# Four graph layers on one core: scales loaded first, a series on GpSimd, a direct spread, a branch hint and new ranks

## The chip, the cores and the metric

The kernel runs on one core of a Trainium2 chip. A core has a TensorE (PE) for matrix products, a VectorE (DVE), a ScalarE (ACT), a GpSimd (POOL) and a SyncE (SP); they run side by side, each through its own list of instructions in order, and wait for each other by semaphores. Operands lie in SBUF, products of the PE go to PSUM, and transfers between DRAM and SBUF are issued by SP or POOL. The metric is the time of one execution in microseconds (us) on the device.

## The reference

There are 4096 nodes with 64 features `x`, and an adjacency matrix `adj` of 4096 x 4096 with entries 0 and 1 (about 32 ones in a row). Four layers follow, and each adds its result to `x`; ahead of each the features go through a layer norm and a relu:

```python
h = max(layernorm(x), 0)
# layer 0: a decaying sum over the last 100 neighbours of each node
rank = cumsum(adj != 0, axis=1); k = min(rank[:, -1:], 100)
x += (mask * where(pos > 0, 0.5 ** (k - pos), 0)) @ (h @ W) + b      # pos = rank - (deg - k)
# layer 1: hyperbolic attention; lorentz_linear = linear map, sigmoid(first) * exp(scale) + 1.1, a rescaling
att = adj * sigmoid((2 + 2 * (qm @ k.T)) / att_scale + att_bias)
x += normalised(att @ lorentz_linear(h))
# layer 2: two gated steps, each m = adj @ (x @ W), then a GRU cell (sigmoid, sigmoid, tanh), then relu
# layer 3: hyperbolic midpoint: num = adj @ (gamma * X), den = adj @ (gamma - 1),
#          then artanh, a scaling by the row's sum, tanh, and relu in the tangent space
```

## The kernel before

`fast_kernel` (L916) assumes entries of 0 and 1 and tests that they are; `general_kernel` (L39) computes any input. After the fast kernel has written its output, its flag is loaded on every engine, and `tc.If(others > 0)` (L1910) runs the general kernel if an assumption did not hold. With these inputs it does not run: every engine branches over it.

**Tiles.** The nodes stand in 4 quarters (`q`) of 1024 and in 32 row blocks (`b`) of 128. The adjacency, transposed, is loaded once by POOL's queue and turned into an 8-bit float on the way: 65 transfers `A<-in_adjT`, seven ahead, 256 KB each when they land, and it stays in SBUF for all four layers.

**Who sets the order.** `Plan` (L636) collects operations with a cost per engine, what they need, what they write, and a rank (`prio`). `Plan.order` (L790) then runs through time as a model: at each step it takes, on the engine that can begin earliest, the operation with the lowest rank, and it chooses between ACT and DVE where both are allowed. Its constants (`HOP`, `FROM_PE`, `SWITCH`, `NEAR`, `WAIT`, `TURN`, `LOAD` and others, from L640) are the model's hops between engines and penalties; the dictionary `K` (L912) holds ranks and a few counts. The result is written out under `tc.manual_schedule()` (L1825), so on the chip each engine works in that order, whatever the real times are.

**Layer 0** (`layer0`, `block0`, L1215 and L1231). The rank of a neighbour is counted in PSUM: each row block adds a triangle matrix times its 128 x 1024 piece of the adjacency (`tri`, operand `ftri`), and a second product (`upd`, `fupd`) completes the count. Between the two, `weigh` reads the counts and makes the decaying weights from them, on ACT (L1275) or DVE (L1277). A quarter's block is done in two halves of 512 columns, so two chains count, weigh, update, count run side by side: 4 x 32 x 2 = 256 weighs in all. A third product (`add`) sums the features with the weights. All products are issued from one helper line, L1047; transposes from L1056.

**Layer 1** (`pre1`, `open1`, `stream1`, `post1`). `pre1` makes the vectors, the keys and the queries of a quarter, transposed. The 128 x 512 queries are written to DRAM (`qS`, `qs<-m`) and `open1` reads them back in four transfers, so that each half of the features lies on both halves of the partitions. `stream1` then goes over 16 pairs of row blocks: a score is eight products into one PSUM tile of 128 x 1024, ACT takes the sigmoid (L1025), DVE multiplies by the adjacency (L983), and PE adds the products. `es` (the exponentials of the scales), `att_mul` and `att_add` come from a slice `scales` of the constants `W`. `W` (456.5 KB) is loaded by SP after some adjacency transfers; `later_consts` (L1130) then computes them and `deep`, a value that the tests need, and the gates' biases.

**Layers 2 and 3.** `stream2` and `gates` do the two gated steps. `pre3` prepares layer 3, `stream3` (L1666) sums over the neighbours for a unit of half a quarter (four column blocks, eight units), and `post3` (L1686) finishes the units in the groups (0, 1, 2), (3, 4, 5), (6, 7). `kept` units have the first two quarters' sum taken early by `kept3` and the rest later. Powers (inverse roots) run on POOL (`root`, L1010). `artanh2` (L1584) takes two logarithms on ACT and, for small arguments, a series of six DVE operations; it is called seven times, four in `pre3` and three in `post3`.

**Tests.** All of `adj` is also read as 32-bit floats in 128 transfers of 512 KB and tested to be exactly 0 or 1, by one DVE operation (L1200) or two sigmoids on ACT (L1204, L1205). `K["tests"]` of them are tied to places in layer 1, the others come after it.

Of the kernel before, what the change touches and what calls it, by code (L numbers as in the profile page):

```python
# [9 lines left out]
F32 = mybir.dt.float32  # L10
# [3 lines left out]
ALU = mybir.AluOpType  # L14
# [621 lines left out]
class Plan:  # L636
# [4 lines left out]
    TO_PE = 0.055  # L641
    FROM_PE = 0.21
    SWITCH = 0.11
    TABLE = 1.3
# [3 lines left out]
    FIRST = 1.2  # L648
    NEAR = 0.396
    WAIT = 1.892  # L650
    TURN = 0.355
    LOAD = 0.136

# [121 lines left out]
    def drop(self, b):  # L775
# [7 lines left out]
        elif b.kind != "fixed":  # L783
# [3 lines left out]
            for j in range(b.units):  # L787
                self.ps[i + j] = t

    def order(self, nst):  # L790
        self.nst = nst
# [13 lines left out]
        def est(o, e):  # L805
            t = 0.0
            for d in o.needs:
                hop = (0.0 if d.on == e and not d.nbytes else self.FROM_PE if d.on == "PE" else
                       self.TO_PE if e == "PE" else self.HOP)
                t = max(t, d.end + hop)  # L810
            return t
# [9 lines left out]
        while len(placed) < len(self.ops):  # L821
# [39 lines left out]
            if o.mode:  # L861
                d += self.SWITCH if o.mode != mode else 0.0
                mode = o.mode
# [47 lines left out]

K = {"lags": (32, 32, 32), "two": (0, 1, 2, 3), "p0": (0.779, 0.744, 1.253, 0.665), "p1": (1.588, 1.422, 1.181, 2.145), "ahead": 7, "early": 0, "steps": ((0, 0, 16), (1, 0, 16), (2, 0, 16), (3, 0, 16)), "score": (3.0, 3.0, 2.571, 3.0), "add": (3.1, 3.971, 4.33, 3.215), "p2": ((0.42, 0.267, 0.42, 0.43), (0.48, 0.272, 0.42, 0.204)), "l2": (4.0, 4.857), "l3": 6.0, "tests": 31, "act": 0, "g": (5, 6), "stage": (5, 8), "cnt": 2, "weigh": 0.164, "sum": 1.612, "kept": 4, "units": ((0, 1, 2), (3, 4, 5), (6, 7)), "p3": (0.541, 0.329, 0.157)}  # L912


@with_exitstack
def fast_kernel(ctx: ExitStack, tc: tile.TileContext, t: dict, out: bass.AP, flag: bass.AP):  # L916
# [92 lines left out]

    def root(o, a, power, n=QB, prio=2.0, cost=2.45):  # L1010
        return plan.op({"POOL": cost + 0.157 * (n - QB)},
                       lambda e: G_.tensor_tensor(o.get(), a.get(), POWER[power].get().to_broadcast([P, n]), ALU.pow),  # L1012
                       (a, POWER[power]), (o,), prio)
# [77 lines left out]
    ones16 = const.tile([P, 1], BF16, name="ones16")  # L1091
    tiny = const.tile([P, 1], F32, name="tiny")
    tiny16 = const.tile([P, 2], F16, name="tiny16")
    tiny8 = const.tile([P, 2], F8, name="tiny8")
# [17 lines left out]

    def first_consts():
        V.memset(powers[:, 0:1], -0.5)
        V.memset(powers[:, 1:2], 0.5)
        V.memset(ones, 1.0)
        V.memset(ones16, 1.0)
        V.memset(tiny, TINY)
        V.memset(tiny8.bitcast(U8), 1)
        V.memset(half16, 0.5)  # L1120
        V.memset(mean16, 1.0 / P)
        V.memset(odd, 0.0)
        V.memset(deep[:, 0:1], -DEEP)
        V.memset(deep[:, 1:2], -BIG2 - DEEP)
        after = sb_tiles[NSB - 1][:, P:2 * P]
        V.tensor_scalar(after, diff, 0.0, None, op0=ALU.is_gt)
        V.scalar_tensor_tensor(tri, ident, 256.0 - MAX_NEIGH, after, op0=ALU.mult, op1=ALU.add)
        V.tensor_scalar(upd, tri, -1.0, 1.0, op0=ALU.mult, op1=ALU.add)

    def later_consts():  # L1130
        S_.activation(es, w("scales", 0, 3), AF.Exp)
        S_.activation(deep[:, 2:3], deep[:, 0:1], AF.Sigmoid)
        V.reciprocal(deep[:, 2:3], deep[:, 2:3])
        V.reciprocal(att_mul, w("scales", 4, 5))
        V.tensor_scalar(att_mul, att_mul, 2.0, None, op0=ALU.mult)
        V.tensor_tensor(att_add, att_mul, w("scales", 3, 4), ALU.add)
        for i in (1, 2):
            V.tensor_tensor(gate_b[:, 3 * i - 3:3 * i - 1], w(f"gb{i}", 0, 2), w(f"gb{i}", 3, 5), ALU.add)
            V.tensor_scalar(gate_b[:, 3 * i - 1:3 * i], gate_b[:, 3 * i - 2:3 * i - 1], -1.0, None, op0=ALU.mult)
# [162 lines left out]

    S1, kT, qS = {}, {}, {}

    def pre1(q, prio):
# [70 lines left out]
        qT = sb(2, "qT")  # L1376
        copy(qT, turn4(flat(y), prio), prio=prio)
        d = dram.tile([P, CW], F32, name=f"qs{q}")
        qS[q] = fixed(d)
# [7 lines left out]
    def open1(q):  # L1387
        qd = []
        for c in range(2):
            v = sb(2, "qd")  # L1390
            for r in range(2):
                half = slice(r * D, (r + 1) * D)
                dma(v.part(r)[half, :], View(qS[q].buf, lambda c=c: qS[q].get()[c * D:(c + 1) * D, :]), D * CW * 4, 1.0,
                    after=ends.get(("qd", q), ()))
            qd.append(v)
        return qd, [bank("acc1")] if q < EARLY else [bank("acc") for _ in range(2)]

    def stream1(q, qd, acc, steps):
        early = len(acc) == 1
        for i in steps:  # L1400
            gs = []
            for c in range(2):
                ps = bank("sc", 2)

                def score(e, i=i, c=c, ps=ps):
                    kb = kT[i // 4].get()[:, (i % 4) * P:(i % 4 + 1) * P]
                    o = ps.get().rearrange("p (j n) -> p j n", j=2)
                    for h in range(2):
                        for j in range(2):
                            half = slice(j * D, (j + 1) * D)  # L1410
                            mm(o[h * D:(h + 1) * D, j, :], kb[half, h * D:(h + 1) * D], qd[c].get()[half, :])
                scores.append(plan.op({"PE": 0.856}, score, (kT[i // 4], qd[c]), (ps,), K["score"][q], "corner", after=scores[-1:]))
                g = sb(4, "g")
                fn(g, ps, AF.Sigmoid, 1280, 1.0, "sig", View(attv.buf, lambda: att_add), View(attv.buf, lambda: att_mul))
                g3 = g.re("p (j n) -> p j n", j=2)
                m = g.re("p (k n) -> p k n", n=P)
                tt(m, m, A[q][i].bits(U8).re("p j (k c n) -> p c (j k) n", c=2, n=P)[:, c], ALU.mult, 2 * CW, 1.0)
                gs.append(g3)
            for j in range(2):
                def add(e, i=i, j=j, gs=gs):  # L1420
# [6 lines left out]
                    for r in range(2):  # L1427
                        half = slice(r * D, (r + 1) * D)
                        for c in range(2):
                            mm(acc[r].get()[c * D:(c + 1) * D, :], s[half, :], gs[c].get()[half, j, :], b == 0, b == NB - 1)  # L1430
                ends[1, q, i] = plan.op({"PE": 0.856}, add, (*gs, S1[(2 * i) // QB]), tuple(acc), K['add'][q],
                                           "narrow" if early else "corner")

    def post1(q, acc, prio):
# [13 lines left out]
        r = stat()  # L1448
        root(r, s, -0.5, prio=prio, cost=1.9)
        v = nodes("att")  # L1450
        tt(v, sup, rows(r), ALU.mult, prio=prio)
        tt(X[q], X[q], v, ALU.add, prio=prio)
        g = nodes("g0")
        relu_ln(X[q], g, prio, 1.9)
        HL[0, q] = two(f"hl0_{q}")
# [127 lines left out]

    def artanh2(x, n, prio):  # L1584

# [5 lines left out]
        x2 = stat(n)  # L1591
        tt(x2, xc, xc, ALU.mult, n, prio)
        p = stat(n)
        ts(p, x2, 2.0 / 9, None, ALU.mult, n=n, prio=prio)
        for k in (7, 5, 3):
            stt(p, p, 2.0 / k, x2, ALU.add, ALU.mult, n, prio)
        stt(p, p, 2.0, xc, ALU.add, ALU.mult, n, prio)
        low = stat(n).bits(I32)
        ts(low, xc, 0.18, None, ALU.is_lt, n=n, prio=prio)
        tt(q, up, q, ALU.subtract, n, prio)  # L1600
# [85 lines left out]
    def post3(units, banks, kept, prio):  # L1686
# [35 lines left out]
        tt(n, n, rd, ALU.mult, nb, prio)  # L1722
        a = artanh2(n, nb, prio)
        part = stat(nb)
# [16 lines left out]

    plan.op({"POOL": 0.75}, lambda e: pool_consts(), (), (identv,), 1.0)
    plan.op({"DVE": 1.2}, lambda e: first_consts(), (identv,), (triv, pv), 0.0)

# [11 lines left out]
    def load_consts(after, behind):  # L1756
        gate(Wv, lambda: W[:1, :1], behind)
        dma(Wv, View(None, lambda: t["consts"][:, :L.at["scales"].stop]), P * L.at["scales"].stop * 4, 0.1, after=after)
        for q in range(NQ):
            bias0(q)  # L1760
        plan.op({"DVE": 1.5}, lambda e: later_consts(), (Wv,), (esv, attv, gbv), 3.0)
        subnormals(3.0)
# [26 lines left out]
    for k, (b, q) in enumerate(left):  # L1789
        if k < early:  # L1790
            turn = 2 + k * (NQ * NB // 2 - 2) // early
            turn = (ends[1, turn // (NB // 2), turn % (NB // 2)],)
            later_test(b, q, turn, {"DVE": 1.31, "ACT": 2.35} if k % 8 < K["act"] else {"DVE": 1.31})
        else:
            later_test(b, q, (ends[1, NQ - 1, NB // 2 - 1],), {"DVE": 1.31, "ACT": 2.35})

# [3 lines left out]
    def verdict(e):  # L1800
# [11 lines left out]
        V.tensor_scalar(both.get(), both.get(), float(n), None, op0=ALU.not_equal)  # L1812
    plan.op({"DVE": 1.4}, verdict, (*tested_, esv), (both,), 0.2)
    keys = [-1, -3, *range(NQ * NB), *(f"g{q}" for q in range(NQ)), *(f"n{us[0]}" for us in K["units"])]
# [4 lines left out]
    def count_odd(e):  # L1819
        mm(fl.get()[:1, :1], total.get(), ones, True, False)  # L1820
        mm(fl.get()[:1, :1], both.get(), ones, False, True)
    plan.op({"PE": 0.2}, count_odd, (total, both), (fl,), 0.2, "full")
    plan.op({"DVE": 0.2}, lambda e: V.tensor_copy(flag, fl.get()[:1, :1]), (fl,), (), 0.2)

    with tc.manual_schedule():  # L1825
        for o in plan.order(NST):
            o.emit(o.on)
    return plan
# [85 lines left out]
```

## Time and profile before

| | |
|---|---|
| runs of the kernel | median 654.51 us (654.39 to 654.60, 3 runs) |
| the profiled execution | 654.29 us, span 652.5 us |
| mean granted TensorE clock | 0.986 |
| busy, share of the span | PE 604.3 us (93%), DVE 518.7 (79%), ACT 432.2 (66%), POOL 123.7 (19%) |
| DMA | 93.6 MB in 33020 packets, mean 143 GB/s |

The profile shows one execution: for every instruction its engine, its line and its duration, and for idle time the instruction or transfer whose end released the engine. The span goes from the first instruction to the last. "Busy" counts an engine's work and not its waits. "PE" is the matrix products and "PEld" the loading of their weights, which overlaps them. A release is inferred from the semaphore that came last. SPq, DVEq and the like are the sequencers of the engines, which issue transfers and take branches.

### The profile page before, as it was taken

Reading aid. Unit: us, or ns where it says so; the run is one execution under the profiler, and the core shown is the slowest. Engines: PE = TensorE matmul, PEld = TensorE weight load, DVE = VectorE, ACT = ScalarE, POOL = GpSimd, SP = SyncE. Lnnn points to the kernel's source line nnn. Section 1 sums busy time; section 2 is a strip of 40 time slices with the busy share of each in tenths; the row PEclk is TensorE's granted clock in tenths of the full one; section 3 lists DMA queues with packets and bytes.
Section 4 is the critical chain, followed back from the end, with each engine's and each line's share of the span. In section 5 each row is a group of like instructions: output and inputs, shape, how many; then the busy total and the mean of one; then the engine's idle time right before and its main releaser. Section 6 shows DMA issues by size and latency. Waiting matters only on the chain.

```text
span 652.5 us, 15178 instructions
## 1 busy us (share of the span) xinstructions
PE 604.3 (93%) x6236; PEld 320.6 (49%) x6236; DVE 518.7 (79%) x969; ACT 432.2 (66%) x646; POOL 123.7 (19%) x126
## 2 busy tenths in 40 slices
PE   4879999999999999999999999999999999999970
PEld 2646666666643333333333333454444445589970
DVE  5855667766678999998989898888888889887765
ACT  4756676777757667766766666448534999988543
POOL 5422342523113101100110110020000213330222
PEclk9989999999999999999999999999999999999995
DMA  8999999999311242123225242698999886636301
GB/s 111 145 108 107 108 115 136 107 120 107 40 49 33 81 131 66 66 81 114 65 71 142 59 124 69 192 355 297 345 339 328 286 298 220 213 102 205 131 26 45
DMA packets 33020, 93.60 MB, mean 143 GB/s; under 512 B 3888, under 2 KB 4656, under 8 KB 32944
## 3 DMA queue, kind: packets, MB, share of 16 engines
q1 hardware_dynamic: 23584, 75.78, 35.4%
q0 software_dynamic: 9360, 16.78, 25.8%
q8 instruction: 51, 0.84, 0.5%
q14 instruction: 25, 0.20, 0.1%
HBM read 138.68 MB, written 2.10 MB: 216 GB/s over the span
## 4 chain that ended last, share of the span: by engine, by line
PE 78%; DVE 9%; ACT 6%; DMA 3%; issue 2%; POOL 1%; DVEq 0%; ACTq 0%; SPq 0%; POOLq 0%
PE p L1047 75%; ACT m L1275 4%; DVE m L1277 3%; PE p L1056 3%; DVE m L983 2%; ACT m L1025 2%; DMA m<-in_x_pm 1%; DVE m L1000 1%; POOL s L1012 1%; DMA m<-in_adjT 1%; DVE s L1005 1%; DMA A<-in_adjT 1%; DVE s L1000 0%; ACT junk L1204 0%; DVE s L983 0%
## 5 line engine op out<-in xcount | busy, mean ns | idle before, releaser
L1047 PE MATMUL p<-m,m 64*64 64x512 f32 (+2 forms) x2538 | 318.8, 555 | 0.6 <-ACT m L1025 0.4
L1025 ACT ACTIVATE m<-p,fatt_add,fatt_mul 128x1024 f32<-128x1024 f32 x128 | 149.8, 1201 | 68.9 <-PE p L1047 66.6
L1012 POOL TENSOR_TENSOR s<-s,powers 128x8 f32<-128x8 f32 (+1 forms) x46 | 87.1, 1903 | 465.7 <-DVE s L994 209.5
L983 DVE TENSOR_TENSOR m<-m,A 128x1024 f32<-128x1024 f32 x128 | 152.8, 1221 | 16.9 <-ACT m L1025 16.2
L1047 PEld LDWEIGHTS p<-m,m 64*64 64x64 f32 x2072 | 79.1, 132 | 145.0 <-issue 97.4
L1275 ACT ACTIVATE m<-p 128x512 int16<-128x512 int8 x168 | 97.3, 596 | 56.8 <-PE p L1047 53.2
L1200 DVE SCALAR_TENSOR_TENSOR junk<-m 128x1024 uint8<-128x1024 f32 x97 | 118.4, 1220 | 1.9 <-DMA m<-in_adjT 0.6
L1047 PEld LDWEIGHTS <-m 128*64 128x64 f16 x1536 | 87.8, 110 | 61.7 <-issue 13.3
L1047 PE MATMUL p<-A,m 128*64 128x512 fp8e4 x1024 | 115.2, 380 | 0.0
L1277 DVE TENSOR_SCALAR m<-p 128x512 int16<-128x512 int8 x88 | 60.5, 690 | 40.3 <-PE p L1047 38.8
L1047 PE MATMUL p<-A,fupd 128*64 128x256 f16 x496 | 71.6, 288 | 15.7 <-ACT m L1275 6.6
L1047 PEld LDWEIGHTS <-fupd 128*64 128x64 bf16 x496 | 46.9, 111 | 58.5 <-issue 46.4
L1047 PE MATMUL p<-A,ftri 128*64 128x256 f16 x512 | 72.5, 281 | 3.0 <-DMA A<-in_adjT 3.0
L1047 PE MATMUL p<-m,A 128*128 128x132 f16 x1024 | 62.5, 220 | 4.6 <-ACT m L1025 3.0
L1047 PEld LDWEIGHTS <-A 128*128 128x128 fp8e4 x1024 | 60.3, 96 | 8.1 <-issue 8.0
L1025 ACT ACTIVATE m<-m 128x512 f32<-128x512 f32 (+4 forms) x69 | 38.9, 580 | 15.6 <-DVE m L983 10.8
L1025 ACT ACTIVATE m<-p 128x512 f32<-128x512 f32 (+4 forms) x40 | 19.2, 485 | 44.3 <-PE p L1047 39.1
L1005 DVE TENSOR_REDUCE s<-m 128x8 f32<-128x512 f32 (+2 forms) x62 | 42.9, 694 | 4.0 <-DMA m<-in_x_pm 2.0
L1043 POOL DMA_DIRECT2D A<-in_adjT x65 | 35.4, 554 | 30.6 <-DMA A<-in_adjT 29.8
L1047 PEld LDWEIGHTS <-ftri 128*64 128x64 bf16 x512 | 34.8, 111 | 6.7 <-issue 4.4
L1204 ACT ACTIVATE junk<-m,deep 128x1024 uint8<-128x1024 f32 x31 | 35.4, 1143 | 2.6 <-DVE junk L1200 2.5
L1205 ACT ACTIVATE junk<-m,deep 128x1024 uint8<-128x1024 f32 x31 | 35.6, 1149 | 1.0
(106 smaller groups left out, 358.3 us busy)
## 6 DMA issues: line engine op xcount, KB each, us to landing
m<-in_adjT SPq DMA_DIRECT2D x128, 512.0 KB, 5.6
A<-in_adjT POOLq DMA_DIRECT2D x63, 256.0 KB, 17.9
m<-qs SPq DMA_DIRECT2D x16, 128.0 KB, 4.7
m<-m SPq DMA_DIRECT2D x16, 128.0 KB, 4.8
m<-in_x_pm SPq DMA_DIRECT2D x4, 256.0 KB, 7.5
qs<-m SPq DMA_DIRECT2D x4, 256.0 KB, 5.0
out_x<-m SPq DMA_DIRECT2D x3, 256.0 KB, 2.1
m<-in_consts SPq DMA_DIRECT2D x2, 256.0 KB, 3.2
```

Of the source, the lines that this page charges most:

```text
L983: return plan.op(cost or {"DVE": dve(n)}, lambda e: ENG[e].tensor_tensor(o.get(), a.get(), b.get(), op), (a, b), (o,), prio)
L1005: return plan.op({"DVE": dve(n)}, lambda e: V.tensor_reduce(o.get(), a.get(), AX.X, ALU.add), (a,), (o,), prio)
L1012: lambda e: G_.tensor_tensor(o.get(), a.get(), POWER[power].get().to_broadcast([P, n]), ALU.pow),
L1025: S_.activation(o.get(), a.get(), func, **k)
L1043: return plan.op({eng: 0.06 if eng == "SP" else 0.55}, lambda e: ENG[e].dma_start(o.get(), a.get()), (a,), (o,), prio, nbytes=nbytes, afte ...
L1047: nc.tensor.matmul(o, lhsT, rhs, start=start, stop=stop, skip_group_check=True)
L1056: nc.tensor.transpose(o[:, j * P:(j + 1) * P], s[:, j * P:(j + 1) * P], ident)
L1200: V.scalar_tensor_tensor(junk, s.get(), 0.0, s.get(), op0=ALU.not_equal, op1=ALU.not_equal, accum_out=odd[:, i:i + 1])
L1204: S_.activation(junk2, s.get(), AF.Sigmoid, bias=deep[:, 0:1], scale=-BIG0, accum_out=zeros[:, k:k + 1])
L1205: S_.activation(junk2, s.get(), AF.Sigmoid, bias=deep[:, 1:2], scale=BIG2, accum_out=ones_of[:, k:k + 1])
L1275: S_.activation(o, s, AF.Relu, scale=-128.0)
L1277: V.tensor_scalar(o, s, -128.0, 0.0, op0=ALU.mult, op1=ALU.max)
```

## The change

Five things are changed.

1. **Scales first.** The five columns of scales have an SBUF tile of their own and an SP transfer ahead of all others. The constants are made in other groups: `plain_consts` (memsets), `first_consts` (`tri`, `upd`), `scale_consts` (ACT: the exponential and a sigmoid), `other_consts` (DVE: `deep`, `att_mul`, `att_add`) and `gate_consts` (the biases, still after `W`). One more activation, an exponential into `deep[:, 3:4]`, stands ahead of them.
2. **The series of `artanh2` on GpSimd.** Nine small POOL operations in place of six on DVE, in all seven calls (`K["series"]`).
3. **Queries of quarter 0 spread directly**, by four transfers from SBUF to SBUF, without the DRAM tile (`K["direct"]`). The other quarters go by DRAM as before.
4. **A branch hint.** The plan is written out in two parts, and between them, ahead of one DVE operation of the last artanh, each engine gets a hint that the branch of the `If` named "general" is likely taken.
5. **The planner's constants and ranks** have new values: hops from PE and mode switches by kind, `NEAR`, `WAIT`, `LOAD`; nearly all ranks in `K`; early tests 26 instead of 31, one in eight of them allowed on ACT; `kept` from unit 5 on instead of 4; the cost it takes for `root` 1.8 instead of 2.45. The flag's product (`count_odd`) comes after all of `stream3`. With `half` at (0, 0) the attention's sigmoid and product stay whole.

```diff
-    FROM_PE = 0.21
-    SWITCH = 0.11
+    FROM_PE = {"n": 0.22, "f": 0.23, "c": 0.31}
+    TO_DVE = 0.07
+    SWITCH = {"fn": 0.11, "nf": 0.11, "fc": 0.14, "cf": 0.11, "cn": 0.16, "nc": 0.1}
...
-    NEAR = 0.396
-    WAIT = 1.892
+    NEAR = 0.377
+    WAIT = 2.312
     TURN = 0.355
-    LOAD = 0.136
+    LOAD = 0.0
...
-K = {"lags": (32, 32, 32), "two": (0, 1, 2, 3), "p0": (0.779, 0.744, 1.253, 0.665), "p1": (1.588, 1.422, 1.181, 2.145), "ahead": 7, "early": 0, "steps": ((0, 0, 16), (1, 0, 16), (2, 0, 16), (3, 0, 16)), "score": (3.0, 3.0, 2.571, 3.0), "add": (3.1, 3.971, 4.33, 3.215), "p2": ((0.42, 0.267, 0.42, 0.43), (0.48, 0.272, 0.42, 0.204)), "l2": (4.0, 4.857), "l3": 6.0, "tests": 31, "act": 0, "g": (5, 6), "stage": (5, 8), "cnt": 2, "weigh": 0.164, "sum": 1.612, "kept": 4, "units": ((0, 1, 2), (3, 4, 5), (6, 7)), "p3": (0.541, 0.329, 0.157)}
+K = {"lags": (32, 32, 32), "two": (0, 1, 2, 3), "p0": (1.395, 2.467, 1.194, 0.878), "p1": (1.588, 2.782, 1.98, 2.145), "ahead": 7, "early": 0, "steps": ((0, 0, 16), (1, 0, 16), (2, 0, 16), (3, 0, 16)), "score": (3.0, 2.67, 2.571, 1.915), "add": (3.044, 3.971, 3.193, 3.818), "p2": ((0.42, 0.267, 0.42, 0.43), (0.245, 0.272, 0.42, 0.204)), "l2": (4.46, 4.857), "l3": 5.448, "tests": 26, "act": 1, "g": (5, 6), "stage": (5, 8), "cnt": 2, "weigh": 0.05, "sum": 3.161, "kept": 5, "units": ((0, 1, 2), (3, 4, 5), (6, 7)), "p3": (0.294, 0.187, 0.416), "direct": (0,), "half": (0, 0), "soft": (1.661, 1.0, 1.0, 1.622), "series": 1}
...
-    def later_consts():
-        S_.activation(es, w("scales", 0, 3), AF.Exp)
+    def scale_consts():
+        S_.activation(es, scales[:, 0:3], AF.Exp)
         S_.activation(deep[:, 2:3], deep[:, 0:1], AF.Sigmoid)
...
+    def spread(rows_of, prio, after=()):
+        qd = []
+        for c in range(2):
+            v = sb(2, "qd")
+            for r in range(2):
+                dma(v.part(r)[r * D:(r + 1) * D, :], rows_of(c), D * CW * 4, prio, after=after)
+            qd.append(v)
+        return qd
...
+        if q in K["direct"]:
+            qD[q] = spread(lambda c: View(qT.buf, lambda: qT.get()[c * D:(c + 1) * D, :]), prio)
+            return
...
+        def series(e):
+            o, s, s2 = p.get(), xc.get(), x2.get()
+            G_.tensor_tensor(s2, s, s, ALU.mult)
+            G_.tensor_scalar(o, s2, 2.0 / 9, 2.0 / 7, op0=ALU.mult, op1=ALU.add)
+            for k in (5, 3, 1):
+                G_.tensor_tensor(o, o, s2, ALU.mult)
+                G_.tensor_scalar(o, o, 2.0 / k, None, op0=ALU.add)
+            G_.tensor_tensor(o, o, s, ALU.mult)
+        if K["series"]:
+            plan.op({"POOL": 2.2}, series, (xc,), (x2, p), prio)
...
+    scalesv, deepv, edgev = fixed(scales), fixed(deep), fixed(tiny8)
+    dma(scalesv, View(None, lambda: t["consts"][:, L.at["scales"]]), P * 5 * 4, 0.0)
...
+    plan.op({"ACT": 1.5}, lambda e: S_.activation(deep[:, 3:4], deep[:, 0:1], AF.Exp), (deepv,), (deepv.part(3),), 0.0)
...
+    plan.op({"ACT": 1.7}, lambda e: scale_consts(), (deepv, scalesv), (esv, deepv.part(2)), 0.0)
+    plan.op({"DVE": 0.6}, lambda e: other_consts(), (deepv.part(2), scalesv), (attv, deepv.part(4)), 0.01)
...
+    for part in (placed[:at], placed[at:]):
+        if part[0] is plan.mark:
+            tc.no_sync_barrier()
+            tc.mark_branch_hint_location("general", "LikelyTaken", engines=engines)
+            tc.no_sync_barrier()
...
-            with tc.If(others > 0):
+            with tc.If(others > 0, label="general"):
```

## The prediction

> **What bounds the kernel now.** I read the chain of work that ended last, cut the span into stages by a table of windows, and then looked in each stage for what the PE waits on. The chain is 78% PE, so a change off the PE counts only where the PE stands still, or after its last work. Columns of the table: window, its length, busy us (instructions) of PE, PE weight loads, DVE, ACT, POOL, then granted clock, DMA share and GB/s.
>
> ```profile
> 43.00:182.00 139.00, 129.78 (x1528) 86.62 (x1531) 89.86 (x176) 95.08 (x171) 42.79 (x55) 1.00 0.97 105
> 219.00:435.00 216.00, 215.99 (x1962) 77.40 (x1954) 195.05 (x237) 141.53 (x145) 17.42 (x8) 1.00 0.36 108
> 562.00:634.00 72.00, 66.57 (x1066) 62.37 (x1063) 54.24 (x168) 48.24 (x93) 17.37 (x13) 1.00 0.40 129
> 634.00:652.00 18.00, 0.24 (x4) 0.14 (x4) 11.35 (x53) 6.47 (x14) 5.52 (x4) 0.59 0.12 41
> ```
>
> From 219 to 435 us (attention) the PE is busy without a gap: no rank or constant shortens it, only fewer matmuls would. Room is in four places: layer 0 (0 to 182), layer 3's stream (562 to 634), the tail on DVE and ACT (634 to 646.5), and the end behind the branch. Layer 0 first, where the timeline shows one broad hole:
>
> ```profile
> 36.36 1.28 ACT L1132 ACT_TABLE_LOAD   x1
> ...
> 37.89 0.16 DVE L1133 RECIPROCAL deep<-deep 128x1 f32<-128x1 f32 x1 [2.23 <-ACT deep L1132]
> ...
> 38.40 0.30 PE L1047 MATMUL p<-A,fupd 128*64 128x256 f16 x2 [1.67 <-ACT m L1275]
> ...
> 38.94 0.69 DVE L1277 TENSOR_SCALAR m<-p 128x512 int16<-128x512 int8 x1
> 39.01 0.53 POOL L1043 DMA_DIRECT2D A<-in_adjT  x1 [1.92 <-DMA A<-in_adjT]
> ```
>
> ACT loads a table, DVE waits for the constant behind it and then makes eight small ones, and no count is weighed; the PE, which needs each weigh before the next update, stands 1.67 us. The last line is the other limit: the POOL issues the next adjacency transfer every 1.92 + 0.53 = 2.45 us, when one has landed. The last of the 65 lands at 171.0; with four weighs on it, 0.65 apart, the last weigh can start at 173.6 at the earliest, and in the timeline it starts at 181.3. So layer 0 can gain 7.7 us at most, whatever the order.
>
> **The sum, part by part** (against the profiled execution, 654.29 us, span 652.5; the median of the runs, 654.51, is 0.2 higher, which I add at the end).
>
> *Scales first.* The Exp and its table, deep and its table, and the small DVE operations move ahead of the first weigh, which ACT begins at 6.2 us after standing idle 3.99. Moved onto ACT there: a second load of 1.28 and three activations of 0.20, hidden if the scales have landed by about 4.5. SP issues one more DMA ahead of x, 0.33 us; the first count waits for an A transfer from the POOL queue (1.34 us, released at 5.77), not for x. The hole goes: the 1.67 of PE idle, and with it the rise of the lag (from a tile's landing to its first weigh) from 0.5 us up to 34 us to 2.0 at 38. I take −2.0. Next late is the DMA: at 0.5 lag the chain waits for transfers again.
>
> *Ranks, layer 0.* ACT's weighs go from 168 to 201, DVE's from 88 to 55; the two rows are
>
> ```profile
> L1275 ACT ACTIVATE m<-p 128x512 int16<-128x512 int8 x168 | 97.3, 596 | 56.8 <-PE p L1047 53.2
> L1277 DVE TENSOR_SCALAR m<-p 128x512 int16<-128x512 int8 x88 | 60.5, 690 | 40.3 <-PE p L1047 38.8
> ```
>
> (last: busy us, mean ns | idle before, releaser). 33 × (0.690 − 0.596) = 3.1 us less weighing, shared by the two half-blocks that run side by side: −1.5. Layer 0: −3.5. Bounds: −1.5 (the hole only, the lag won being lost again) to −7.7, the DMA floor. Above zero only by the slower rival.
>
> *Work of the PE behind layer 0.* Matmuls are the same in number and shape. In the changed order 123 scores instead of 125 are left behind the last count, and 26 groups of four transposes instead of 24. A score of eight matmuls takes 0.86 (250.50 to 251.36 in the timeline), four transposes 0.44 (573.12 to 573.56): −1.72 + 0.88 = −0.8. One more switch between tile shapes there, about 0.1. Layer 2's gates: the PE's waits (0.34 to 0.77, six of them) lie at much the same places; −0.3, between 0 and −0.6.
>
> *Ranks, layer 3.* Ten times the PE waits for ACT or DVE to read the very PSUM bank that it filled last, since the next product is ordered into it:
>
> ```profile
> 620.40 3.89 PE L1047 MATMUL p<-m,A 128*128 128x132 f16 x64 [0.52 <-DVE m L983]
> 624.82 3.90 PE L1047 MATMUL p<-m,A 128*128 128x132 f16 x64 [0.52 <-DVE m L983]
> 629.23 4.36 PE L1047 MATMUL p<-m,A 128*128 128x132 f16 x72 [0.52 <-DVE m L983]
> ```
>
> Starts 4.41 apart where 64 × 0.061 = 3.89 is work: 0.52 each here, 0.53 to 0.69 with the refilling of the array (mean 0.62). The new order has three left (in the last third); the other seven save 7 × 0.62 = 4.4; two that still stand close (a pass of 17 matmuls between) may cost 0.25 each. I take −3.9, between −2.2 (half) and −4.4.
>
> *Last artanh on POOL.* From the last product (633.6) to the last output issue (646.5) DVE runs a chain of small operations, 0.17 long, 0.20 apart. Six per artanh leave DVE; nine on POOL take their place, beside two Ln on ACT. No row has a small arithmetic POOL operation. The nearest:
>
> ```profile
> L1012 POOL TENSOR_TENSOR s<-s,powers 128x8 f32<-128x8 f32 x42 | 78.1, 1868 | 424.1 <-DVE s L994 209.5 <-DVE s L983 154.2 <-DVE s L1000 51.1
> L1012 POOL TENSOR_TENSOR s<-s,powers 128x12 f32<-128x12 f32 x4 | 9.0, 2264 | 41.6 <-DVE s L992 41.6
> L1660 POOL MEMSET m<- 128x8 f16 x8 | 0.8, 105 | 20.3 <-ACT m L1025 14.3 <-PE p L1047 5.1 <-ACT junk L1205 0.5
> ```
>
> Lower end: the memset of the same shape, 0.105, nine of them 0.95. Upper end: the power's fixed part. In undisturbed instances 8 columns take 1.63 and 12 take 2.26, so 0.157 a column, 0.4 fixed: 9 × 0.43 = 3.9. I take 0.22, by the iota of 128 columns (0.238), which is a plain POOL operation and so nearest: 2.0 us. The tail's groups of four blocks no longer share their tables: four loads of 1.28 instead of two, partly beside the DVE chain. Following the new order operation by operation gives 12.3 instead of 12.9: −0.5, with −0.7 and +3.3 at the ends. Here a rule speaks against the change: the Trainium skill, "GPSIMD Engine Reference", section 3.1, keeps elementwise work on DVE, with a GpSimd tensor_tensor 1.96 times as long as DVE's at 2048 columns; by that my estimate would be 9 × 0.34 = 3.1 us and +1.3 for this term. No row of this trace shows it.
>
> *Branch hint.* Columns: engine, operation, count, ns min/median/max, first and last start:
>
> ```profile
> L1910 SPq EVENT_SEMAPHORE  x8: 17/17/17, 650.3 to 650.8; - x8
> ...
> L1910 DVEq COMPARE_BRANCH  x1: 72/72/72, 646.1 to 646.1; - x1
> L1910 SPq COMPARE_BRANCH  x1: 50/50/50, 647.5 to 647.5; - x1
> L1910 DVEq EVENT_SEMAPHORE  x1: 21/21/21, 649.1 to 649.1; - x1
> ```
>
> From branch to next instruction SP takes 2.8 us and DVE 3.0, doing nothing; SP's lie on the end. The last output, issued at 646.5, lands at 649.1. With the target already at hand SP waits for that landing instead: 650.3 becomes about 648.8, −1.5 (end −1.8 if the landing is quick, 0 if the hint is not followed). The Trainium skill, "Runtime: NRT & Kernel Launch", section "Instruction fetch mechanics", says that a taken branch out of the fetched window fetches the target first; the 2.8 us agree, and it names no hint, by which this term would be 0.
>
> *Queries spread without DRAM.* One write and a wait for it go, for quarter 0, whose queries are needed at 182; the PE then has other scores and is never idle to 435. Nothing; if that cover went, the write's 5.0 us landing.
>
> *Sum.* −3.5 − 0.8 + 0.1 − 0.3 − 3.9 − 0.5 − 1.5 = −10.4: 643.9, with the 0.2 **644.1**.
>
> **Rivals.**
> 1. *Layer 0 comes down to the DMA floor.* −7.7 instead of −3.5: 639.9. For it: lag only 0.5 us until the hole, and it grows from there. Against: a dip of the granted clock (0.83 from 34 to 43 us) is behind part of it, and the PE is 93% busy from 43 to 182.
> 2. *Part of it only.* Hint not followed (+1.5), POOL series at 0.43 each (+3.8), layer 0 with the hole alone (+2.0): single ones give 645.6, 647.9, 646.1, all three 651.4. For it: POOL's rows are all dear.
> 3. *Slower: weighing crowds ACT.* 33 more weighs at 0.60 stand behind the other half's weigh or another activation: 19.8 us over two chains, 9.9, less 2.0 for the hole. Layer 0 then +7.9, total 655.5. It decides once the last weigh starts 6.9 us later than now, after 188.2. For it: the PE's waits on ACT weighs are the longer ones (13 of 6.6 us, on DVE 16 of 4.0). Against: ACT stood idle 56.8 us before its weighs, waiting for the PE.
> 4. *The changes cancel* within 0.2% (1.3 us, about what a measurement of this kernel tells from nothing).
>
> **How the numbers follow.** Likeliest, 641.5 to 647: 0.48. DMA floor, 638.5 to 641.5: 0.14. Part only, 647 to 653: 0.23. Same: 0.04. Slower: 0.11. Faster is 0.48 + 0.14 + 0.23 = 0.85. The range runs from 638.5 (floor, with the better ends of the tail and the end) to 652 (all three failings, and half a us), and leaves out slower, same and the rest of the third, about 0.18.
>
> **What would show it.** Right: last weigh at about 177.8; no table load and no DVE wait near 36 to 39 us; three PE waits of some 0.5 us in layer 3's stream, not ten; POOL operations of about 0.22 in the tail and 12.3 us from last product to last output issue; the instruction behind SP's branch under 1.5 us after it. Wrong: a last weigh after 188; POOL operations over 0.4; first weigh later than 6.5 because the scales land late; the 2.8 us still there.

## The result and the profile after

The changed kernel takes **651.34 us** (median of 5 runs, 651.13 to 652.01) where the kernel before took 654.39 beside it: a ratio of 0.9955, 95% interval 0.9945 to 0.9966. The forecast was 644.1 us, a gain of 10.4; the gain is 3.0. The span went from 652.5 to 649.5 us, and four marks of the two traces, all in us from the span's start, say where:

| mark | before | after | gained or lost since the mark above | forecast |
|---|---|---|---|---|
| last product of layer 3 begins | 633.37 | 628.54 | -4.83 | -8.4 |
| last output transfer is issued | 646.49 | 642.63 | +0.97 | -0.5 |
| SP's first instruction behind its branch | 650.30 | 646.25 | -0.19 | -1.5 |
| end of the span | 652.50 | 649.55 | +1.10 | (in the -1.5) |

So the PE came 4.8 us earlier to its end, and 1.9 of it was given back behind it. The four stages follow in the same view as before (columns: window, length, busy us of PE, weight loads, DVE, ACT, POOL, clock, DMA share, GB/s; the last window is shorter):

```profile
43.00:182.00 139.00, 130.68 (x1536) 84.44 (x1535) 72.00 (x148) 108.30 (x196) 40.39 (x55) 1.00 0.96 101
219.00:435.00 216.00, 216.00 (x1966) 80.07 (x1959) 191.02 (x230) 142.57 (x148) 17.37 (x8) 1.00 0.35 108
562.00:634.00 72.00, 64.25 (x1047) 61.24 (x1044) 57.24 (x169) 51.51 (x98) 30.09 (x49) 0.99 0.47 148
634.00:649.00 15.00, 0.00 (x0) 0.00 (x0) 5.58 (x21) 4.13 (x9) 5.41 (x11) 0.50 0.14 48
```

In layer 0 DVE works 18 us less and ACT 13 more, attention is as full as before, and from 562 us on POOL works 30 us instead of 17. The waits of the PE in layer 3 (window 545 to 629; columns: waiting line and its releaser, us in total, times, longest):

```profile
PE p L1053 <- DVE m L989: 1.1, 3, 0.5
PE p L1053 <- POOL m L1700: 1.0, 1, 1.0
PE p L1062 <- DVE m L998: 0.8, 1, 0.8
PE p L1053 <- ACT m L1031: 0.7, 2, 0.4
```

Before, the same view (548 to 634) had eight waits on ACT and three on DVE:

```profile
PE p L1047 <- ACT m L1025: 3.5, 8, 0.5
PE p L1047 <- DVE m L983: 1.6, 3, 0.5
```

All but one of these eleven are the waits on a PSUM bank that the prediction counted; the other one is between scores. Now five waits on a bank are left, 1.8 us in all, but 1.0 on POOL and 0.8 on DVE (L998) are new. At the end, the branch (count, ns min/median/max, first and last start):

```profile
L1965 SPq EVENT_SEMAPHORE  x8: 17/17/17, 646.3 to 646.8; - x8
...
L1965 DVEq COMPARE_BRANCH  x1: 84/84/84, 642.5 to 642.5; - x1
L1965 SPq COMPARE_BRANCH  x1: 70/70/70, 643.6 to 643.6; - x1
...
L1965 DVEq EVENT_SEMAPHORE  x1: 21/21/21, 645.4 to 645.4; - x1
```

SP still stands for 2.65 us behind its branch and DVE for 2.88: 2.83 and 2.99 before.

### The profile page after: what moved, and what is told of

It is laid out like the page before. It is cut to its first block, busy times and chain, and to the rows that moved or that the text cites. A ratio compares the mean times of both kernels' runs of the same rounds, so it can differ in the third digit from the quotient of the medians.

```text
span 649.5 us, 15174 instructions
## 1 busy us (share of the span) xinstructions
PE 602.9 (93%) x6236; PEld 319.1 (49%) x6236; DVE 493.5 (76%) x898; ACT 445.6 (69%) x671; POOL 144.3 (22%) x189
## 5 line engine op out<-in xcount | busy, mean ns | idle before, releaser
L1053 PE MATMUL p<-m,m 64*64 64x512 f32 (+1 forms) x2600 | 322.6, 555 | 0.9 <-DVE m L1042 0.7
L1053 PEld LDWEIGHTS p<-m,m 64*64 64x64 f32 (+1 forms) x2128 | 81.2, 132 | 145.4 <-issue 104.3
L1288 ACT ACTIVATE m<-p 128x512 int16<-128x512 int8 x201 | 113.9, 596 | 40.0 <-PE p L1053 34.8
L1213 DVE SCALAR_TENSOR_TENSOR junk<-m 128x1024 uint8<-128x1024 f32 x98 | 119.7, 1221 | 3.4 <-DMA m<-in_adjT 2.2
L1290 DVE TENSOR_SCALAR m<-p 128x512 int16<-128x512 int8 x55 | 37.7, 690 | 43.3 <-PE p L1053 37.8
L1217 ACT ACTIVATE junk<-m,deep 128x1024 uint8<-128x1024 f32 x30 | 34.3, 1142 | 2.6 <-DMA m<-in_adjT 2.4
L1218 ACT ACTIVATE junk<-m,deep 128x1024 uint8<-128x1024 f32 x30 | 34.5, 1149 | 1.0
```

Source lines behind the costliest of these rows:

```text
L1053: nc.tensor.matmul(o, lhsT, rhs, start=start, stop=stop, skip_group_check=True)
L1213: V.scalar_tensor_tensor(junk, s.get(), 0.0, s.get(), op0=ALU.not_equal, op1=ALU.not_equal, accum_out=odd[:, i:i + 1])
L1217: S_.activation(junk2, s.get(), AF.Sigmoid, bias=deep[:, 0:1], scale=-BIG0, accum_out=zeros[:, k:k + 1])
L1218: S_.activation(junk2, s.get(), AF.Sigmoid, bias=deep[:, 1:2], scale=BIG2, accum_out=ones_of[:, k:k + 1])
L1288: S_.activation(o, s, AF.Relu, scale=-128.0)
L1290: V.tensor_scalar(o, s, -128.0, 0.0, op0=ALU.mult, op1=ALU.max)
```

## The experiments

The theory made from these traces, called A in the expectations: the hint saves nothing, the series on POOL costs more than DVE's six operations, the hole in layer 0 was worth what was forecast, and the ranks make the rest. The rivals stand with each run. "Same places" means that the planned order was kept and only the named operations changed; the other kernels were planned anew. Intervals are those of the ratio to the kernel before on the same chip.

**The hint.** The three calls that place it are taken out, and the plan is written out in one piece.

```diff
-            tc.no_sync_barrier()
-            tc.mark_branch_hint_location("general", "LikelyTaken", engines=engines)
-            tc.no_sync_barrier()
```

> The changed kernel (median 651.34 us) without the five hints, nothing else. Theory A (the hint does nothing on SP): SP still takes about 2.65 us from its branch to its next instruction, the time stays within 0.3 us of 651.34; POOL's branch, short in the changed kernel (0.2 us), is short for another reason and stays short. Rival (the hint is followed, and what it saves shows on POOL): POOL's branch goes back to the 1.9 us of before, and SP's gap grows from 2.65 towards 2.83; the time is 0.2 to 1.5 us longer.

651.02 us, 0.9951 (0.9937 to 0.9964). From branch to next instruction SP takes 2.67 us, ACT 2.42, DVE 3.12, PE 3.93 and POOL 0.18: with the hint 2.65, 2.53, 2.88, 3.59 and 0.20. So A. The hint saves nothing that can be told from the scatter, though ACT and DVE pass it 6.8 us ahead of their branch: the best kernel below has no hint either, and DVE takes 2.92 and PE 3.75 there. POOL's 1.9 us in the kernel before was no cost of the branch: POOL's last power ended at 640.65, and its next instruction came at 640.68.

**The branch laid out to fall through.**

```diff
-            with tc.If(others > 0, label="general"):
+            with tc.If(others > 0, label="general", preferred_fallthrough_block=False):
```

> The changed kernel with the branch laid out so that not running the general kernel falls through, and an unconditional jump over the general kernel comes after SP's waits for its output transfers. Theory A (a jump out of the fetched page costs about 2.7 us wherever it stands): SP's next instruction follows its branch within 0.3 us, then it waits for the last output's landing, then jumps for 2.7 us: 0 to 2 us longer than 651.34. Rival (an unconditional jump is seen ahead and fetched early): the end is shorter by 1.5 to 2.5 us.

653.62 us, 0.9986 (0.9977 to 0.9995). The branch itself costs 0.12 us on SP now, but the jump over the general kernel follows at 646.0, behind the landing, and takes 2.8 us: A. The cost stays with the jump that leaves out the general kernel, wherever it stands. The kernel is 2.3 us longer than the changed one, a little over A's 0 to 2; 0.45 of it is SP's second stop (next experiment), which is 1.42 us long here.

**Where the code lies.** In the changed kernel SP's last work has a hole of 0.97 us ahead of a drain (647.57 to 648.55), which before had not.

```diff
+    spare = const.tile([P, 64], F32, name="spare")
+    for i in range(64):
+        nc.sync.dma_start(spare[:, i:i + 1], t["x"][:P, i:i + 1])
```

(in the general kernel, which does not run)

> The changed kernel with 64 more SP transfers inside the general kernel, which does not run: the executed instructions are the same, only the code behind the branch lies 64 SP instructions further on. Theory A (the 0.97 us ahead of SP's drain at the end is a second fetch of code, at a border that falls between the branch's target and the drain): the gap goes, and the time is 0.8 to 1.1 us shorter, about 650.4. Rival (the drain waits for something that runs, a transfer or another engine): the gap stays, 651.0 to 651.6.

649.71 us, 0.9933 (0.9919 to 0.9947), and the hole is gone. The drains of SP in the changed kernel and in this one (the same program line, moved):

```profile
L1960 SPq DRAIN  x3: 7/7/122, 648.5 to 649.0; - x3
```

```profile
L1964 SPq DRAIN  x3: 7/7/13, 646.9 to 647.3; - x3
```

The first drain follows SP's jump target (646.25 and 645.58) by 2.30 us in the one and by 1.36 in the other. A second sign that it is a matter of the place in the code: counted in the trace, such a hole of 0.8 to 1.1 us stands ahead of SP's 354th instruction in ten profiles here of the changed code without the padding, and ahead of the 355th in the one with the branch laid out to fall through; the kernel before has only 353. That SP fetches code there is the reading of A; the traces show the stop and its place. The other 0.6 of the 1.6 us lies ahead of it: the last product begins at 627.91, with nothing in the edit to explain it. It is within the scatter: five profiles of this same order have that product between 627.91 and 628.99.

**The series on DVE at POOL's places.**

```diff
-            G_.tensor_tensor(s2, s, s, ALU.mult)
...
+            V.tensor_tensor(s2, s, s, ALU.mult)
+            V.tensor_scalar(o, s2, 2.0 / 9, None, op0=ALU.mult)
+            for k in (7, 5, 3):
+                V.scalar_tensor_tensor(o, o, 2.0 / k, s2, op0=ALU.add, op1=ALU.mult)
+            V.scalar_tensor_tensor(o, o, 2.0, s, op0=ALU.add, op1=ALU.mult)
```

> The changed kernel with the series of all seven artanh on DVE again (six operations), at the places in the order that POOL had. Theory A (the series is what lengthens the tail): nine POOL operations at a pitch of 0.31 us, 2.7 to 3.3 us in the chain, become six on DVE at 0.20, 1.2 us, partly on top of the DVE's own chain; the tail of 13.9 us from the last product to the last output issue falls by 0.8 to 2.0, and the 0.96 us for which the PE waited on a POOL memset behind a series goes too: about 649 us. Rival (the tail is DVE work, and the longer tail comes from its new grouping and table loads): taking 1.2 us more onto DVE makes it longer, 651.5 to 652.5 us.

649.27 us, 0.9921 (0.9907 to 0.9934), 2.1 less than the changed kernel: A. The tail, from the last product's begin to the last output issue, falls from 14.09 to 13.29 us, and the PE's last product comes 1.24 earlier (627.30): both new waits of the PE in layer 3, on POOL (0.96) and on DVE's L998 (0.78), are gone, and one of 0.54 has come. The tail in the changed kernel (timeline of POOL, then the DVE operation that waits for it):

```profile
633.58 3.27 POOL L1018 TENSOR_TENSOR s<-s,powers 128x8 f32<-128x8 f32 x2
636.81 0.38 POOL L1622 TENSOR_TENSOR s<-s 128x8 f32<-128x8 f32 x1
637.27 0.37 POOL L1623 TENSOR_SCALAR s<-s 128x8 f32<-128x8 f32 x1
637.73 0.52 POOL L1625 TENSOR_TENSOR s<-s,s 128x8 f32<-128x8 f32 x1
638.34 0.24 POOL L1626 TENSOR_SCALAR s<-s 128x8 f32<-128x8 f32 x1
...
639.89 0.20 POOL L1627 TENSOR_TENSOR s<-s,s 128x8 f32<-128x8 f32 x1
...
640.13 0.17 DVE L1641 COPY_PREDICATED s<-s,s 128x8 f32<-128x8 int32 x1 [1.58 <-POOL s L1627]
```

Three costs are to be seen: the series stands behind two powers; its operations are 0.20 to 0.24 long but 0.31 apart, and longer beside DVE; and DVE waits 1.58 us at its end. With the series on DVE that operation comes at 638.10, 1.2 after the last of the six.

**The same, planned anew** with `"series": 0`.

> The changed kernel with the series on DVE and the order planned for that, so every operation may shift. Theory A (the ranks were fitted with the series on POOL, but POOL costs more than its place in the order can hide): 648.5 to 650.5 us, no longer than with POOL. Rival (the ranks only fit the order with the series on POOL): over 651.5 us.

651.61 us, 0.9957 (0.9943 to 0.997). That is 0.1 above the rival's bound, which the runs (651.13 to 651.83) do not decide; it is clearly above A's 650.5. The PE ends 2.4 us earlier (626.12), but the tail is 17.0 us; why it is so long was not followed further.

**Only the last series on DVE**, those of the units 0 to 5 on POOL, no hints, padded.

> The kernel without hints, with 64 idle SP instructions in the general kernel and the series on DVE (647.65 us), but with the series of the units 0 to 5 on POOL and only pre3's and the last on DVE. Theory A (only a series that ends on the critical chain costs): the tail is 0.3 to 1.0 us shorter than the 13.3 us with all on DVE, since DVE keeps six operations fewer ahead of the last group: 646.7 to 647.4. Rival (POOL's powers for the last group queue behind the series, as in the changed kernel): 647.6 to 648.5.

649.03 us, 0.9911 (0.9898 to 0.9925). Neither: the tail is 13.36 us, as with all on DVE (13.29). The 1.4 us against the best kernel lie ahead of it (the last weigh already starts 1.1 later), in a part that both share, and are left open.

**Scales late again, at the same places otherwise.** The three operations are moved behind `gate_consts` in the planned list.

```diff
+    placed = [o for o in placed if o not in moved]
+    there = placed.index(behind_w[0])
+    placed[there:there] = moved
```

> The changed kernel with the exponential, its table, deep and the constants from it moved back behind W in the same order, so that ACT loads a table and DVE waits in the middle of layer 0. Theory A (most of layer 0's gain is this hole): the lag of weighs behind landings jumps by about 2 us near 36 us and stays, the time is 1.5 to 2.5 us longer, about 653.3. Rival (layer 0 is bound by PE work or by the transfers, and takes the hole in): the lag at the end is again 8.2 us and the time within 0.5 us of 651.34.

653.21 us, 0.9991 (0.9979 to 1.0002): 1.87 more than the changed kernel, A. The last weigh starts 1.4 later (181.42 instead of 180.02), the last product too. The stretch with the hole, in the kernel before, the changed one and this one:

```profile
34.00:43.00 9.00, 6.46 (x62) 4.07 (x59) 4.32 (x14) 5.78 (x11) 2.11 (x4) 0.83 1.06 108
34.00:43.00 9.00, 7.22 (x80) 4.51 (x80) 5.40 (x13) 7.12 (x14) 3.67 (x5) 1.00 1.06 109
34.00:43.00 9.00, 5.73 (x64) 3.91 (x64) 4.18 (x15) 7.74 (x16) 2.05 (x2) 1.00 1.06 109
```

The granted clock was 0.83 in this stretch of the kernel before and 1.00 with the scales late again, so the 1.87 is the price of the hole without that dip of the clock; what the dip cost the kernel before no run shows.

**Weighs back on DVE.** Every sixth of ACT's weighs, at the same places, beside an unaltered copy on the same chip.

```diff
+    for o in [o for o in placed if o in weighs and o.on == "ACT"][3::6]:
+        o.on = "DVE"
```

> The changed kernel with every sixth of ACT's 201 weighs given to DVE at the same place in the order, so that ACT has about 167 and DVE 89 again, as before. Theory A (a weigh on ACT rather than DVE is worth what the prediction gave it, 1.5 us for 33): the last weigh starts 1 to 2 us later than in the unchanged copy run beside it, the time is 1 to 2 us longer. Rival (layer 0 is bound by the PE's own work and the arrival of tiles, the weighs' engine matters little): the same within 0.5 us. Second rival (ACT was crowded): 0.5 us or more shorter.

> The changed kernel itself, unaltered, beside the kernel with 33 weighs given back to DVE on the same chip: both theories expect 651.3 us, within 0.5.

657.29 us, 1.0056 (1.0042 to 1.007), and the copy 651.59. The last weigh starts at 185.98 instead of 180.43. The direction is A's, the size nearly four times its. The waits of the PE from 0 to 182 us, weighs given back and copy:

```profile
PE p L1053 <- DVE m L1292: 8.6, 24, 1.3
PE p L1053 <- ACT m L1290: 3.6, 10, 0.6
```

```profile
PE p L1053 <- ACT m L1288: 4.8, 14, 0.6
...
PE p L1053 <- DVE m L1290: 2.6, 8, 0.7
```

A weigh that is handed to DVE in an order made for ACT also queues behind what DVE has there. So relieving ACT does not help in this order, and the size says nothing on an order made for 88 weighs on DVE.

**The old ranks.** The changed code with the constants, costs and `K` of before.

> The changed kernel's code (scales first, series on POOL, direct spread, hints) planned with the constants, costs and ranks of the kernel before. Theory A (of the 4.8 us that the PE is ahead at its last product, 1.9 are the hole, and the ranks make the rest): the PE ends some 2 to 3 us later than in the changed kernel, about ten waits of 0.4 to 0.5 us stand in layer 3's stream again, and the time is 653 to 655.5 us. Rival (the new ranks make the tail and give nothing in sum): 650.5 to 651.5 us, with two table loads fewer in the tail.

658.13 us, 1.006 (1.0047 to 1.0074), 3.8 slower than the kernel before: beyond what either theory expected. And with its series on DVE at the same places:

> The kernel with the old ranks (658.13 us) with its series on DVE at the same places. Theory A (it is the series on POOL that makes the old order 3.8 us slower than the kernel before: POOL operations held up by DVE, and what stands behind them in POOL's order): 654 to 656 us. Rival (the order as planned is worse, whoever computes the series): 657 to 659 us.

657.23 us, 1.0041 (1.0027 to 1.0054). The rival: the order itself is worse. With the old ranks the last weigh starts at 180.61, 0.7 us earlier than in the kernel before, so the scales loaded first are worth less in that order than in the new one; but layer 2's last product comes at 564.5 instead of 560.2. Of the 6.8 us between old and new ranks in this code, 3.8 only bring it back to the time of the kernel before. Which rank does it stays open.

**The direct spread.** `"direct": ()`, planned anew.

> The changed kernel with the queries of quarter 0 by DRAM again, planned anew. Theory A (hidden behind other scores, as the prediction said): 650.8 to 651.9 us, the PE without a gap from 219 us on. Rival (the write and its landing are on the path at the start of attention): 1.5 us or more longer, with a PE gap near 182 to 219 us.

651.54 us, 0.9953 (0.9939 to 0.9967), the PE full from 182 to 435: A, worth nothing that can be told, though the new plan shifts other operations too (200 weighs on ACT instead of 201).

**The best of it:** no hints, series on DVE at the same places, padded.

> The changed kernel without hints, with the series on DVE at the same places, and with the 64 idle SP instructions in the general kernel. Theory A: the time of the kernel with the series on DVE, 649.3, less the 0.85 us gap ahead of SP's drain: 648.4. Rival (gap not a matter of where the code lies): 649.0 to 649.5.

**647.65 us, 0.9897 (0.9882 to 0.9912)**, 6.6 less than before and less than the sum expected. The tail is 13.29 us, and SP has no hole.

**Its last output by POOL.**

> The kernel of 647.65 us with its last output transfer issued by POOL instead of SP, so that SP branches after the last but one transfer. Theory A (SP's jump of 2.7 us stands on the path, and lies beside the last DVE operations then): the end waits for DVE's own jump (2.9 us from 640.2) and for the landing: 0.5 to 1.3 us shorter, 646.3 to 647.1. Rival (a transfer by POOL lands later by more than the jump): 648 us or more.

649.46 us, 0.9922 (0.9909 to 0.9936). The rival's time, but not by its mechanism. SP does branch early (639.4) and comes to its second drain at 644.8, and the transfer lands in 2.7 us, like SP's of this size (2.8). POOL now branches last, at 642.0, and its drain, which takes 5.4 us behind the branch in the kernel before and the changed one too and lay hidden there, ends at 647.7.

## Why the prediction was wrong, point by point

- *What bounds the kernel*: right. Attention stayed full, and all that moved lies in the four places named.
- *Scales first, -2.0*: right in the new order, 1.87 by the kernel with late scales. The scales landed in time: ACT takes their exponential at 2.50 us, and its second table load ends at 3.99.

```profile
2.50 0.20 ACT L1140 ACTIVATE es<-scales 128x3 f32<-128x3 f32 x1 [0.18 <-DMA scales<-in_consts]
2.71 1.28 ACT L1141 ACT_TABLE_LOAD   x1
```

- *Ranks, layer 0, and the PE's work behind it, together -2.2*: too large. By 182 us the PE has done 2.4 us more than before (busy 162.2 against 159.7), so hole and ranks give 2.4 together, and the ranks some 0.5. The waits on weighs fell by the 3.5 us that layer 0 was priced at, from 10.6 us to 7.1. But the weighs, 3.6 us ahead at the 193rd (136.2 against 139.8), are 1.1 ahead at the 221st and 0.2 to 0.4 from the 237th to the 251st, and the last one starts at 180.0, 1.3 earlier and not at 177.8. In that stretch the new order puts a linear map and a sigmoid of attention (1.20 us) between the weighs:

```profile
155.26 0.60 ACT L1288 ACTIVATE m<-p 128x512 int16<-128x512 int8 x1 [0.51 <-PE p L1053]
156.31 1.20 ACT L1031 ACTIVATE m<-p,fatt_add,fatt_mul 128x1024 f32<-128x1024 f32 x1 [0.45 <-PE p L1053]
157.87 1.69 ACT L1288 ACTIVATE m<-p 128x512 int16<-128x512 int8 x3 [0.36 <-DMA qs<-m]
```

  ACT weighs at 155.3 and next at 157.9. Before, three such sigmoids stood between the weighs as well, but earlier (114.3, 141.0 and 143.7), and none from there to 182.7. Whether this costs the 1.7 us that is missing was not tried; ACT's work other than weighs from 148 to 176 us is no more than before (4.1 us against 4.3), so the cause stays open.
- *Layer 2's gates, -0.3*: not so. The PE's six waits between 182 and 545 us are 2.65 us in all, 2.2 before.
- *Ranks, layer 3, -3.9*: the step that failed by most. Of the ten waits on banks five went, not seven, and each of the five that are left costs 0.2 to 0.5. That is 2.8 us less of idle; counted from start to start as the forecast did (its 0.62 each; 7 times that is 4.3 and not 4.4), it is 3.6, close to the 3.9. What failed is that the forecast put nothing down for waits that the new order makes: two of them took 1.7 of idle back (2.2 by the forecast's measure), so that the stage won 1.1 to 1.4 us. One of the two is POOL's:

```profile
581.69 1.23 DVE L1213 SCALAR_TENSOR_TENSOR junk<-m 128x1024 uint8<-128x1024 f32 x1
581.79 1.18 POOL L1623 TENSOR_SCALAR s<-s 128x8 f32<-128x8 f32 x1
...
583.03 1.22 DVE L1213 SCALAR_TENSOR_TENSOR junk<-m 128x1024 uint8<-128x1024 f32 x1
583.06 1.25 POOL L1625 TENSOR_TENSOR s<-s,s 128x8 f32<-128x8 f32 x1
...
586.08 0.22 POOL L1700 MEMSET m<- 128x8 f16 x4
586.18 0.17 DVE L1641 COPY_PREDICATED s<-s,s 128x8 f32<-128x8 int32 x1 [1.91 <-POOL m L1700]
586.24 1.97 PE L1053 MATMUL p<-m,A 128*128 128x132 f16 x31 [0.96 <-POOL m L1700]
```

  The small memset that layer 3's products need stands behind the series on POOL, and the series lasts 4.9 us here, not 2.0. With the series on DVE both waits are gone (0.54 came elsewhere). I had asked what waits for the series, and not what is queued behind it.
- *Series, 2.0 us and a tail of -0.5*: wrong in size. The duration was right, 0.20 to 0.24 where nothing disturbs; a product of two tensors takes 0.20 on POOL and 0.16 to 0.17 on DVE, a ratio of 1.2 at 8 columns, so the price of 0.34 that I weighed against it did not come. But I multiplied the duration without the gaps (0.31 from start to start, 2.8 us in all), and took POOL to be free and undisturbed; measured in the last call, 3.3 us behind two powers of 1.6. The +1.3 that I gave for 0.34 each was also wrong by my own working: the upper end of +3.3 counts both calls of the tail, and so counted 0.34 gives +1.7. The tail became 0.97 longer. With the series on DVE it is 13.29, 0.2 longer than before, so the new grouping with four table loads brought no gain of its own either.
- *Hint, -1.5*: wrong; "not followed" was the case. The 0.97 behind it, SP's second stop, was in none of my bounds: I had taken the end sequence behind the jump as fixed at 2.2 us.
- *Spread*: right, nothing.
- *Rival 3, ACT crowded*: refuted. The last weigh starts at 180.0 and not after 188.2, and weighs handed back to DVE make it 5.6 us later, not earlier.

By the marks: the PE's end fell short by 3.6 us, the tail by 1.5 and the end by 2.4; these are the 7.4 us between 10.4 and 3.0. Of the 4.8 us that were won at the PE's end, 2.4 were won by 182 us, and 1.0 is idle time less behind it (3.2 of the waits in layer 3, less the two new ones and the gates). The other 1.3 us is busy time less for the same number of products (602.9 instead of 604.3), which was not followed. The second rival, a part of it only, was the case, 0.7 us inside the range's upper end. That its sum, 651.4, meets the measured time is luck: the hint failed as it says, but the series cost less than its 3.8 us, and SP's second stop and layer 3's new waits, which are not in it, made up the rest.

## What to carry to other kernels

Work moved to an idle engine still has a queue: price the gaps between its operations, what it stands behind, what stands behind it, and what disturbs it. Ranks fitted to one program can be worth little to another (old ranks in the new code: 3.8 us slower than before), so test an edit by changing only its operations at the same places of the order; planned anew, the edit cannot be told from the shuffle. Count the code behind the last branch as time, and look at where it lies.

## What the runs showed of the hardware that was not expected

- **POOL is held up by DVE, operation by operation.** Of the 63 series operations in the changed kernel 48 took 0.20 to 0.26 us. The other 15 took 0.37 to 1.25, and each of these ends 0.06 to 0.11 us behind a DVE operation with two SBUF inputs, as in the lines at 581 to 584 us. A DVE reduction beside them (632.46, 0.69 us) left POOL at 0.24, and so did a DVE product with one of its two inputs in PSUM (567.31, 0.69 us; POOL 0.20 and 0.24). This was seen in the trace and not tested by itself.
- The Trainium skill, "SBUF — State Buffer", section "Who interferes with whom", states just this: a DVE instruction with two SBUF inputs contends with a GpSimd instruction that reads SBUF, the other blocks fully, and a reduction never contends. The trace agrees; this was the rule to weigh against the change.
- **A branch hint changed nothing** in five engines' gaps, 2.4 to 3.9 us on four of them: with and without it they differ by at most 0.34 us, and two kernels that both have it (the changed one and the padded one) by up to 0.46.
- **SP stops a second time shortly behind its jump**, for 0.84 to 1.42 us, and this depends on where the code lies: it goes when code that never runs is made longer (1.36 us instead of 2.30 from the jump's target to the drain). The Trainium skill, "Runtime: NRT & Kernel Launch", section "Instruction fetch mechanics", calls the crossing of a block mostly hidden; close behind a jump it is not, by these runs.
- **POOL's drain at the end takes 5.4 us**, hidden while POOL branches early enough (640.4 against SP's 643.6 in the changed kernel).
